# Layer 1's attention bias: from a 33-row matmul inside the output product to an addition on VectorE

## The chip, the cores and the metric

The kernel runs on one core of one Trainium2 chip. The metric is the device time of one execution in microseconds (us). The core has five engines that run their own instruction streams in order: TensorE (PE, with its weight loads listed apart as PEld), VectorE (DVE), ScalarE (ACT), GpSimd (POOL) and SyncE (SP), which here issues most of the DMAs.[...]

## The reference, cut to what matters

Two transformer-like layers are computed on 4096 tokens of width 256. Layer 0 is a linear attention plus a mixture of 32 experts; layer 1 is a softmax attention of 16 heads plus a mixture of 8 experts. What matters here is where the output bias `Wo_b` of layer 1's attention enters:

```python
def _L1_attn_ref(X, Wq_w, Wq_b, Wo_w, Wo_b, rms_w):
    ...
    O = O @ Wo_w.T + Wo_b
    return pre_X + O
...
xn = _layernorm(x, axis=-1)
x = x + _L1_attn_ref(xn, ...) + _L1_ffn_ref(xn, ...)
```

So the last line adds, for every token, `x + xn + (O @ Wo_w.T) + Wo_b + experts`. The bias is one row of 256 numbers, the same for all tokens, and it can be added at any place of that sum.

## The kernel before, in words

The 4096 tokens are cut into eight groups of 512 (`NG = 8`), each held as a tile of 128 partitions by four rows of 256 (`[P, TT, D]`). The program is a set of Python generators, one for each piece of work of each group. A generator yields `step(engine, cost, ...)` in front of the instructions that it issues. The class `Weave` simulates the engines with these costs, in us, and always takes the step that can begin first; that fixes the order of the instructions on each engine once and for all. A cost in a `step` is therefore no time of the chip, but it moves the order. `need` names events that must have happened, `get` and `put` take and give back buffers, `lat` is a delay until the result is there, `aside` lets the generator's next step begin without waiting for this one.

The pieces that the change and the prediction touch:

- `loads` at the start of layer 1's weights (L1659 to L1669) brings `wq`, `gate1`, `wo`, `bq`, `rms_w`, `gate_b` on SP's queue. `bq`, a row like the bias, is spread over all 128 partitions by its DMA.
- `biased` (L979 to L990) prepares the bias for TensorE: a tile of 33 rows, zero but for row 0 and row 32, holds the bias rounded to the fast matmul type in row 0 and what the rounding left in row 32. A second tile, `ones_r`, holds ones. A matmul of the two, contracted over 33 rows, adds the bias to every token.
- `combine(g)` (L1019 to L1055) closes layer 0 for a group and opens layer 1. It loads the sum so far (`xt`, L1024), adds the four gathered expert rows `yk` (L1027, gathered by POOL at L1012), takes the layer norm, stores the normed rows and their transpose (L1031, L1042), adds the normed rows to `xt` (L1044), computes the router's logits on PE, copies them (L1053) and stores `xt` as the residual of layer 1 (L1055). The router (`route1`), the scatter of the tokens to the experts (`spread`, L566) and the experts of layer 1 (L1158 on) come from there.
- `attended(g)` (L1489 to L1498) is the output product of layer 1's attention. It runs in two passes over the same four blocks of 128 tokens, one for each half of the contraction. In pass `i = 0` each block has the product's two matmul instructions and then the bias matmul; pass `i = 1` has the product alone. Both go through `into` (L865), so their instructions stand at L871.
- `closed1(g)` (L1556) loads the residual back, adds the finished PSUM banks to it by `onto` (L943), and stores it; `finish(g)` and `added` (L1539 to L1574) add the experts' rows `y1k` at the end and write the output.

The experts of layer 1 run as 39 tiles between the attention of groups 3 to 6; the attention of group 7 and all of `finish` come last.

Of the kernel before, what the change touches and what calls it, by code (L numbers as in the profile page):

```python
# [7 lines left out]
F32 = mybir.dt.float32  # L8
I32 = mybir.dt.int32
BF16 = mybir.dt.bfloat16  # L10
F32R = mybir.dt.float32r
U32 = mybir.dt.uint32
AF = mybir.ActivationFunctionType
ALU = mybir.AluOpType
# [3 lines left out]
P = 128  # L18
D = 256
# [4 lines left out]
NG = T // GT  # L24
TT = GT // P
# [25 lines left out]
C_ID, C_TRI, C_ONE, C_MASK = 0, 128, 256, 384  # L51
# [155 lines left out]
def step(eng, cost, **o):  # L207
    return eng, cost, o
# [3 lines left out]
def two_layers(  # L212
# [6 lines left out]
    nc = tc.nc  # L219
# [4 lines left out]
    def kc_rows(ap):  # L224
        return ap.rearrange("(k p) n -> p k n", p=P)

    const = ctx.enter_context(tc.tile_pool(name="const", bufs=1))
# [7 lines left out]
    w = Weave(  # L235
        dict(
            big=BIG, mid=MID, s=BANKS, o0=2, o1=1, up=1, pT=2, aT0=1, aT1=1,
            unit=2, xr=3, w=3, mt=2, wc=4, rt=1, pp=2, rt1=1, chunk=4, mix1=2,
            at0=1, at1=1, xr1=3, w1r=3, w1b=3,
        )  # L240
    )

    def big(shape, name, dtype=F32):
        return work.tile(shape, dtype, tag="big", name=name, bufs=BIG)
# [6 lines left out]
    def bank(shape, i=0):  # L251

        n = shape[1] if len(shape) == 2 else shape[1] * shape[2]
        ap = banks[w.ids["s"][i]][: shape[0], :n]
        return ap if len(shape) == 2 else ap.rearrange("p (a b) -> p a b", a=shape[1])
# [5 lines left out]
    cst = const.tile([P, C_END], F32, name="cst")  # L261
# [12 lines left out]
    g1_t = const.tile([P, KC, E1], F32, name="g1")  # L274
    wo_t = const.tile([P, KC, D], F32, name="wo")
    bq_t = const.tile([P, D], F32, name="bq")

    BR = 33
    bo_t = const.tile([BR, D], F32, name="bo")
    bo_r = const.tile([BR, D], F32R, name="bo_r")  # L280
    ones_r = const.tile([BR, P], F32R, name="ones_r")
    rw_t = const.tile([P, KC], F32, name="rw")
    gb_t = const.tile([P, E1], F32, name="gb")

# [55 lines left out]
    def load(name, lat, dst, src, eng=None):  # L340
        return name, lat, dst, src, eng
# [25 lines left out]
    def norms(xt, key, need=lambda t: []):  # L367

        st = few([P, TT, 6], "st")
        mv = few([P, TT, 2], "mv")  # L370
        for t in range(TT):
            yield step("DVE", 0.6, need=need(t))
            nc.vector.bn_stats(st[:, t, :], xt[:, t, :])
            nc.vector.bn_aggr(mv[:, t, :], st[:, t, :])
        yield step("DVE", 0.16)
        var = few([P, TT], "var")
        nc.vector.tensor_scalar(var, mv[:, :, 1], LN_EPS, None, ALU.add)
        yield step("POOL", 1.05, rush=RUSH)
        rstd = few([P, TT], "rstd")
        nc.gpsimd.tensor_tensor(rstd, var, nhalf.to_broadcast([P, TT]), ALU.pow)  # L380
        yield step("DVE", 0.16)
        off = few([P, TT], "nmr")
        nc.vector.scalar_tensor_tensor(off, mv[:, :, 0], -1.0, rstd, ALU.mult, ALU.mult)
        for t in range(TT):
            yield step("ACT", 0.6, get=["big"] if t == 0 else [])
            if t == 0:
                xn = xns[key] = big([P, TT, D], "xn")
            nc.scalar.activation(
                xn[:, t, :], xt[:, t, :], AF.Identity, bias=off[:, t : t + 1],
                scale=rstd[:, t : t + 1],  # L390
            )
        yield step("DVE", 0.5)

        ms = few([P, TT], "ms")
        nc.vector.tensor_tensor(ms, rstd, rstd, ALU.mult)
        nc.vector.tensor_tensor(ms, ms, mv[:, :, 1], ALU.mult)
        nc.vector.tensor_scalar(ms, ms, RMS_EPS, None, ALU.add)
        yield step("POOL", 1.05, aside=True, rush=RUSH, gives=[("rs", key)])
        rss[key] = few([P, TT], "rs", bufs=NG)
        nc.gpsimd.tensor_tensor(rss[key], ms, nhalf.to_broadcast([P, TT]), ALU.pow)  # L400
# [464 lines left out]
    def into(o, n, pairs):  # L865

        done = n_down.get(o, 0)
        n_down[o] = done + 1
        for t in range(2 * len(oTs[o])):
            for i, (lhs, rhs) in enumerate(pairs):  # L870
                nc.tensor.matmul(  # L871
                    oTs[o][t // 2][:, t % 2, :],
                    lhsT=lhs[:, t * P : (t + 1) * P] if lhs.shape[1] > P else lhs,
                    rhs=rhs,
                    start=(done == 0 and t % 2 == 0 and i == 0),
                    stop=(done == n - 1 and t % 2 == 1 and i == len(pairs) - 1),
                )
# [85 lines left out]
    halves, logits, aTs, aPs, ys = {}, {}, {}, {}, {}  # L963
# [12 lines left out]
                wq_t[:, k, :], wq_t[:, k, :], rw_t[:, k : k + 1], None, ALU.mult  # L976
            )

    def biased():  # L979
        yield step("DVE", 0.2)  # L980
        nc.vector.memset(bo_t, 0.0)
        yield step("SP", 0.3, lat=45.0)
        nc.sync.dma_start(bo_t[:1, :], bo)
        nc.sync.dma_start(bo_t[BR - 1 :, :], bo)
        yield step("ACT", 0.4, need=["cst"])
        nc.scalar.copy(bo_r, bo_t)
        nc.scalar.copy(ones_r, cst[:BR, C_ONE : C_ONE + P])
        yield step("DVE", 0.4, gives=["bo_r"])
        last = slice(BR - 1, BR)
        nc.vector.tensor_tensor(bo_r[last, :], bo_t[last, :], bo_r[last, :].bitcast(F32), ALU.subtract)  # L990

    def heads():
        for i in range(2):
            yield step("POOL", 2.0)
            nc.gpsimd.memset(vones[i][:, :, :, DK:], 1.0)
            yield step("POOL", 2.5)
            nc.gpsimd.memset(turned[i], 0.0)
            yield step("POOL", 0.2, gives=["heads"] if i else [])
            nc.gpsimd.memset(turned[i][:, :, :, 0:1], -1.0)
# [19 lines left out]
    def combine(g):  # L1019

        need = [("x1", g, b) for b in range(GT // S)] + ["tiles0"]
        yield step("SP", 0.4, get=["big", "mix1"], need=need, lat=2.5, gives=[("mix1", g)])
        xt = big([P, TT, D], "xt")
        nc.sync.dma_start(xt, midg[g])  # L1024
        for k in range(TOPK0):
            yield step("DVE", 1.22, need=[("y", g, k)], put=["big"])
            nc.vector.tensor_tensor(xt, xt, ys.pop((g, k)), ALU.add)  # L1027
        yield from norms(xt, NG + g)
        xn = xns[NG + g]
        yield step("SP", 0.4, aside=True, lat=2.5, gives=[("rows1", g)])  # L1030
        nc.sync.dma_start(rd1g[g], xn)  # L1031
        for k in range(KC):
            yield step("PE", 0.6, get=["s"] + (["big"] if k == 0 else []))
            if k == 0:
                xnT = big([P, KC, GT], "xnT1")
            tp = bank([P, TT, P])
            for t in range(TT):
                nc.tensor.transpose(tp[:, t, :], xn[:, t, k * P : (k + 1) * P], ident)
            yield step("ACT", 0.6, put=["s"])
            nc.scalar.copy(xnT[:, k, :], tp.rearrange("p t n -> p (t n)"))  # L1040
        yield step("SP", 0.4, aside=True, lat=2.5, gives=[("xnT1", g)])
        nc.sync.dma_start(xnT_d[g], xnT.rearrange("p k n -> p (k n)"))  # L1042
        yield step("DVE", 1.22, aside=True)
        nc.vector.tensor_tensor(xt, xt, xn, ALU.add)  # L1044
        yield step("PE", 2.0, get=["s"], need=["gate1"])
        lg = bank([P, TT, E1])
        for t in range(TT):
            matmul_k(
                lg[:, t, :], lambda k: xnT[:, k, t * P : (t + 1) * P], lambda k: g1_t[:, k, :]
            )  # L1050
        yield step("DVE", 0.2, put=["s", "big", "big"], gives=[("lg", g)])
        logits[g] = few([P, TT, E1], "lgs", bufs=NG)
        nc.vector.tensor_copy(logits[g], lg)  # L1053
        yield step("SP", 0.4, lat=2.5, put=["big", "mix1"], gives=[("res1", g)])
        nc.sync.dma_start(res1g[g], xt)  # L1055
# [430 lines left out]
    WO = KC  # L1486
    NC1 = 2

    def attended(g):  # L1489

        for i in range(WO):
            yield step(
                "PE", 1.75 if i else 2.2,
                need=[("o", NG + g), ("aT", g, 0), ("aT", g, 1), "wo", "bo_r"],
                put=["big"] if i == WO - 1 else [], gives=[("dn1", g, NC1 + i)],
            )
            bias = [] if i else [(ones_r, bo_r)]
            into(NG + g, NC1 + WO, [(aPs[g][:, i, :], wo_t[:, i, :])] + bias)  # L1498

    def chunk(g, c):  # L1500

# [155 lines left out]
    for j in range(4):  # L1657
# [5 lines left out]
            load("gate1", 45.0, g1_t, kc_rows(gate1)),  # L1663
            load("wo", 45.0, wo_t, kc_rows(wo)),
            load("bq", 45.0, bq_t, bq.partition_broadcast(P)),
            load("rms_w", 45.0, rw_t, rms_w),
            load("gate_b", 45.0, gb_t, gate_b.partition_broadcast(P)),
        ]), 50,
    )  # L1669
    w.add(scaled(), 52)  # L1670
    w.add(biased(), 53)
    w.add(heads(), 54)
    w.add(late_ring(), DENSE[-1] + 9)
    for g in range(NG):
# [97 lines left out]
```

## Time and profile before

| | us |
|---|---|
| Time, median of 3 runs (lowest to highest) | 1543.43 (1538.72 to 1546.51) |
| The profiled execution, its own time | 1544.06 |
| Its span, first to last instruction | 1542.3 |
| Granted TensorE clock over the span | 0.971 of full |
| L1044, the addition of the normed rows: 8 instructions | 1.217 each |
| L871, bias matmul with weight load: 32 of each | 0.381 and 0.183 each (medians) |
| L986, L987 on ACT and L981, L990 on DVE (`biased`) | 0.391, 0.296, 0.272, 0.449 |

The eight bias passes of `attended` stand at 906, 1047, 1106, 1185, 1274, 1366, 1460 and 1519 us of the span. The eight L1044 additions stand at 725, 752, 779, 847, 906, 987, 1032 and 1092 us.

How to read such a page: its first part gives each engine's busy time, its second the same over 40 slices of the span. A group's row ends in the idle time of the engine before these instructions and in what ended it. In a timeline each row is the start, the duration, the engine, the line, the operation, what it writes and reads, and the shapes; a bracket at the end is idle time before it with its releaser. Matmuls overlap one another, so the time that a matmul takes from its engine is read from start to start and not from its duration.

### The profile page before, as it was taken

How to read it: one execution, taken by the hardware profiler on the slowest of the kernel's cores; microseconds unless marked ns; L12 is line 12 of the kernel's file. 1: busy time of each engine (PE TensorE's matmuls, PEld its weight loads, DVE VectorE, ACT ScalarE, POOL GpSimd, SP SyncE). 2: the span in 40 equal slices, each digit the busy share in tenths (PEclk: the TensorE clock that was granted, in tenths of full speed). 3: DMA queues.
4: the chain of work that ended last, by engine and by line, in shares of the span. 5: the costliest groups of instructions: out<-in, count | busy, mean ns of one | idle time of the engine just before them, and what ended most of it. 6: DMA issues, size and time to landing. Idle time of an engine off the chain costs nothing.

```text
span 1542.3 us, 27989 instructions
## 1 busy us (share of the span) xinstructions
PE 1421.5 (92%) x9702; PEld 1115.6 (72%) x9702; DVE 907.4 (59%) x2421; ACT 726.1 (47%) x1585; POOL 786.7 (51%) x1062
## 2 busy tenths in 40 slices
PE   5999999999999998799889999999889999999965
PEld 3777787577788876688658888876568887777733
DVE  5987767683322233225776645577757676656662
ACT  4333222435554555433343423354566877867521
POOL 4477677545555555437667444336054655645100
PEclk9999999999999999999879999999999999999977
DMA  9211110138777788964486251325355444544393
GB/s 338 96 56 42 42 29 15 28 113 240 211 241 224 232 232 201 177 169 130 135 120 117 76 157 26 113 92 124 121 126 161 137 145 141 152 146 132 99 304 117
DMA packets 160483, 214.23 MB, mean 139 GB/s; under 512 B 29843, under 2 KB 123797, under 8 KB 160085
## 3 DMA queue, kind: packets, MB, share of 16 engines
q1 hardware_dynamic: 131140, 148.92, 31.7%
q0 software_dynamic: 29200, 63.51, 17.3%
q8 instruction: 77, 1.26, 0.3%
q14 instruction: 66, 0.53, 0.1%
HBM read 137.65 MB, written 70.19 MB: 135 GB/s over the span
## 4 chain that ended last, share of the span: by engine, by line
PE 51%; DMA 15%; DVE 4%; issue 3%; POOL 3%; ACT 2%; SPq 2%; DVEq 0%; POOLq 0%; ACTq 0%
PE bank L894 8%; PE bank L871 8%; DMA xr_ring<-rows_d,who 7%; PE bank L350 6%; PE bank L1184 4%; PE bank L1350 3%; PE bank L1361 3%; PE bank L749 3%; PE bank L1407 3%; PE bank L1426 3%; PE bank L1211 2%; PE bank L731 2%; PE bank L1511 1%; POOL xr_ring L715 1%; DMA y1k<-y 1%
## 5 line engine op out<-in xcount | busy, mean ns | idle before, releaser
L715 POOL DMA_INDIRECT xr_ring<-rows_d,who x190 | 181.2, 954 | 163.7 <-PE bank L731 123.1
L566 POOL DMA_INDIRECT perm<-pairs,at_u x192 | 194.3, 1012 | 98.5 <-issue 33.0
L894 PE MATMUL bank<-yT,wsw 128*128 128x256 f32 x1024 | 238.9, 381 | 0.0
L894 PEld LDWEIGHTS bank<-yT,wsw 128*128 128x128 f32 x1024 | 193.2, 191 | 29.2 <-issue 4.0
L736 DVE COPY xTr<-bank 128x512 f32<-128x512 f32 x95 | 65.1, 687 | 175.6 <-PE bank L731 161.0
L1012 POOL DMA_INDIRECT yk<-y,slots x128 | 133.4, 1042 | 61.2 <-issue 34.3
L1372 DVE TENSOR_REDUCE tops<-bank 128x3 f32<-128x384 f32 x256 | 131.4, 548 | 50.4 <-PE bank L1350 50.2
L1419 ACT ACTIVATE pT<-bank 128x384 f32<-128x384 f32 x256 | 111.7, 495 | 93.4 <-PE bank L1350 89.9
L1232 POOL DMA_INDIRECT y<-ry,to x78 | 79.3, 1017 | 109.1 <-ACT ry L1221 78.3
L871 PE MATMUL bank<-wdn,sg 128*128 128x256 f32 x512 | 125.5, 391 | 5.8 <-DVE sg L920 5.8
L871 PEld LDWEIGHTS bank<-wdn,sg 128*128 128x128 f32 x512 | 98.7, 197 | 24.0 <-DVE sg L920 6.1
L759 ACT ACTIVATE ry<-bank,share 128x256 f32<-128x256 f32 x190 | 79.5, 470 | 69.5 <-PE bank L749 67.9
L350 PE MATMUL bank<-xTr,w_ring 128*128 128x256 f32 x380 | 99.3, 386 | 3.3 <-DMA w_ring<-in_wud 2.1
L749 PE MATMUL bank<-w_ring,ra 128*128 128x256 f32 x380 | 98.2, 382 | 0.0
L916 ACT ACTIVATE sg<-bank 128x512 f32<-128x512 f32 x64 | 38.2, 596 | 127.4 <-PE bank L894 127.3
L1140 POOL DMA_INDIRECT xr<-rows_d,who x78 | 81.3, 1043 | 25.4 <-issue 16.8
L350 PE MATMUL bank<-wqkvsu,xnT 128*128 128x512 f32 (+1 forms) x256 | 91.6, 492 | 0.0
L1361 PE MATMUL bank<-kT,qT 32*128 32x128 f32 (+1 forms) x1024 | 77.3, 368 | 11.3 <-DVE at L534 4.0
L1407 PE MATMUL bank<-qT,kT 32*128 32x256 f32 (+1 forms) x1024 | 70.0, 359 | 15.4 <-DVE tops L1372 12.7
L731 PE MATMUL bank<-cst,xr_ring 128*128 128x128 f32 x380 | 62.8, 280 | 22.8 <-DMA xr_ring<-rows_d,who 20.5
L1184 PE MATMUL bank<-xhi,w_ring 128*88 128x256 f32 x312 | 80.5, 292 | 1.2 <-ACT ry L1221 0.7
L743 ACT ACTIVATE ra<-bank 128x256 f32<-128x256 f32 x95 | 36.4, 383 | 95.3 <-PE bank L350 90.0
(257 smaller groups left out, 3128.0 us busy)
## 6 DMA issues: line engine op xcount, KB each, us to landing
w_ring<-in_wud SPq DMA_DIRECT2D x95, 256.0 KB
y<-ry SPq DMA_DIRECT2D x95, 256.0 KB
w_b<-in_we SPq DMA_DIRECT2D x39, 304.0 KB
rows_d<-xn SPq DMA_DIRECT2D x16, 512.0 KB
xnT<-xnT_d SPq DMA_DIRECT2D x16, 512.0 KB
y1k<-y SPq DMA_DIRECT2D x16, 512.0 KB
x<-in_x SPq DMA_DIRECT2D x8, 512.0 KB
res_d<-x SPq DMA_DIRECT2D x8, 512.0 KB
```

The costliest lines, as they stand in the source:

```text
L350: nc.tensor.matmul(ps_ap, lhsT=lhs(k), rhs=rhs(k), start=(k == 0), stop=(k == KC - 1))
L566: ins = nc.gpsimd.indirect_dma_start(out=la.perm, out_offset=bass.IndirectOffsetOnAxis(ap=la.at_u[:, c : c + 1], axis=0), in_=la.pairs[:, ...
L715: nc.gpsimd.indirect_dma_start(out=xr_ring[:, m % 3, i * D : (i + 1) * D], out_offset=None, in_=rows_d, in_offset=bass.IndirectOffsetOnAxi ...
L749: nc.tensor.matmul(o[:, i, :], lhsT=a[:, i * P : (i + 1) * P], rhs=wt[:, 2 * I0 :], start=True, stop=True,)
L871: nc.tensor.matmul(oTs[o][t // 2][:, t % 2, :], lhsT=lhs[:, t * P : (t + 1) * P] if lhs.shape[1] > P else lhs, rhs=rhs, start=(done == 0 a ...
L894: nc.tensor.matmul(ap[:, i, :], lhsT=w_of[0](i, k), rhs=rhs[:, k, :], start=(i == 0 and k == 0), stop=(i == 1 and k == KC - 1),)
L1012: nc.gpsimd.indirect_dma_start(out=ys[g, k][:, t, :], out_offset=None, in_=y0, in_offset=bass.IndirectOffsetOnAxis(ap=L0.slots[:, c : c + ...
L1184: nc.tensor.matmul(h[:, c, :], lhsT=w_c(i // 2), rhs=(hi, lo)[i % 2][:, i // 2, :], start=(i == 0), stop=(i == n - 1),)
L1361: nc.tensor.matmul(four[r][:, i * P : i * P + n], lhsT=qT[rows_of(r), c, i * P : (i + 1) * P], rhs=kT[rows_of(r), c, :n], start=(i == 0), ...
L1372: nc.vector.tensor_reduce(tops[b][:, c * 4 + r, :], four[r].rearrange("p (i n) -> p i n", n=P), AX.X, ALU.max,)
L1407: nc.tensor.matmul(four[r][:, q : q + n], lhsT=kT[rows_of(r), c, i * P : (i + 1) * P], rhs=mT[rows_of(r), c, i * P :], start=(i == 0), sto ...
L1419: nc.scalar.activation(pT[:, :, r, :], four[r].rearrange("p (b n) -> p b n", n=P), AF.Exp)
```

## The change

The bias is no longer part of the output product. It is loaded like `bq`, spread over 128 partitions; in `combine(g)`, right behind the addition of the normed rows, a second addition of the same shape on VectorE adds it to the residual, before that is stored. `biased`, its 33-row tiles, its two small DMAs and the 32 bias matmuls go, with the event `bo_r`; the planned cost of pass `i = 0` becomes that of pass `i = 1`.

```diff
-
-    BR = 33
-    bo_t = const.tile([BR, D], F32, name="bo")
-    bo_r = const.tile([BR, D], F32R, name="bo_r")
-    ones_r = const.tile([BR, P], F32R, name="ones_r")
+    bo_t = const.tile([P, D], F32, name="bo")
...
-    def biased():
-        yield step("DVE", 0.2)
-        nc.vector.memset(bo_t, 0.0)
-        yield step("SP", 0.3, lat=45.0)
-        nc.sync.dma_start(bo_t[:1, :], bo)
-        nc.sync.dma_start(bo_t[BR - 1 :, :], bo)
-        yield step("ACT", 0.4, need=["cst"])
-        nc.scalar.copy(bo_r, bo_t)
-        nc.scalar.copy(ones_r, cst[:BR, C_ONE : C_ONE + P])
-        yield step("DVE", 0.4, gives=["bo_r"])
-        last = slice(BR - 1, BR)
-        nc.vector.tensor_tensor(bo_r[last, :], bo_t[last, :], bo_r[last, :].bitcast(F32), ALU.subtract)
-
...
         yield step("DVE", 1.22, aside=True)
         nc.vector.tensor_tensor(xt, xt, xn, ALU.add)
+
+        yield step("DVE", 1.22, aside=True, need=["bo"])
+        nc.vector.tensor_tensor(xt, xt, bo_t.unsqueeze(1).to_broadcast([P, TT, D]), ALU.add)
         yield step("PE", 2.0, get=["s"], need=["gate1"])
...
             yield step(
-                "PE", 1.75 if i else 2.2,
-                need=[("o", NG + g), ("aT", g, 0), ("aT", g, 1), "wo", "bo_r"],
+                "PE", 1.75,
+                need=[("o", NG + g), ("aT", g, 0), ("aT", g, 1), "wo"],
                 put=["big"] if i == WO - 1 else [], gives=[("dn1", g, NC1 + i)],
             )
-            bias = [] if i else [(ones_r, bo_r)]
-            into(NG + g, NC1 + WO, [(aPs[g][:, i, :], wo_t[:, i, :])] + bias)
+            into(NG + g, NC1 + WO, [(aPs[g][:, i, :], wo_t[:, i, :])])
...
             load("bq", 45.0, bq_t, bq.partition_broadcast(P)),
+            load("bo", 45.0, bo_t, bo.partition_broadcast(P)),
...
-    w.add(biased(), 53)
...
-        "bo": a["L1_attn_Wo_b"].reshape(1, D),
+        "bo": a["L1_attn_Wo_b"],
```

## The prediction

> **What bounds the kernel now.** I read the busy shares first, then the busy time by stretches, because both halves of the change sit late in the span.
>
> ```profile
> PE 1421.5 (92%) x9702; PEld 1115.6 (72%) x9702; DVE 907.4 (59%) x2421; ACT 726.1 (47%) x1585; POOL 786.7 (51%) x1062
> ```
>
> TensorE is busy 92% of the span, but an average hides the stages. The windows (length, then busy time of PE, PEld, DVE, ACT, POOL, the clock and the DMA) separate them:
>
> ```profile
> 725.00:900.00 175.00, 159.24 (x1111) 125.08 (x1110) 118.94 (x389) 69.39 (x133) 111.31 (x137) 0.91 0.54 117
> ...
> 814.00:1020.00 206.00, 204.96 (x1422) 167.38 (x1425) 120.96 (x354) 76.33 (x149) 87.44 (x111) 1.00 0.38 97
> 1020.00:1150.00 130.00, 116.40 (x1212) 79.41 (x1212) 90.67 (x286) 71.67 (x147) 57.38 (x79) 0.97 0.45 121
> 1150.00:1462.00 312.00, 305.53 (x2997) 247.14 (x2998) 208.95 (x392) 221.11 (x430) 162.68 (x234) 1.00 0.44 136
> 1462.00:1543.00 81.00, 48.05 (x347) 29.27 (x346) 34.21 (x49) 16.86 (x38) 0.15 (x1) 0.75 0.67 214
> ```
>
> From 814 to 1020 TensorE idles 1 us in 206, from 1150 to 1462 it idles 6.5 in 312: whatever it is spared there moves everything behind it forward. From 1020 to 1150 it idles 13.6 of 130. The last 81 us are a tail of waits. Ahead of 814 lies a stretch where VectorE and the gathers set the pace: the waits of TensorE list 4.0 us for L534 at 756 and 4.6 us for the maxima (L1372) at 795, both held up on VectorE behind an L1027 addition that waits for a DMA.
>
> **What is removed from TensorE.** The timeline of one bias pass and of the pass without a bias, group 5:
>
> ```profile
> 1365.63 0.60 PE L871 MATMUL bank<-wo,aP 128*128 128x256 f32 x2
> 1366.16 0.38 PE L871 MATMUL bank<-bo_r,ones_r 33*128 33x256 f32 x1
> 1366.47 0.70 PE L871 MATMUL bank<-wo,aP 128*128 128x256 f32 x2
> 1367.10 0.38 PE L871 MATMUL bank<-bo_r,ones_r 33*128 33x256 f32 x1
> ...
> 1369.29 0.66 PE L1162 MATMUL bank<-cst,xr 128*128 128x128 f32 x4
> ...
> 1369.79 1.89 PE L871 MATMUL bank<-wo,aP 128*128 128x256 f32 x8
> ...
> 1371.52 1.03 PE L350 MATMUL bank<-wq,xnT 128*128 128x256 f32 x4
> ```
>
> The bias pass holds the engine from 1365.63 to 1369.29, 3.66 us; the other pass from 1369.79 to 1371.52, 1.73 us. The difference, 1.93 us, is four bias matmuls, 0.48 us each, several times the 0.12 us that the 88-row matmuls of L1211 at 1364.73 to 1365.08 take from start to start. The weight-load rows say why:
>
> ```profile
> 1366.16 0.18 PEld L871 LDWEIGHTS bank<-bo_r,ones_r 33*128 33x128 f32 x1 [0.33 <-issue]
> ```
>
> The bias weights are not loaded during the matmul ahead; the loader idles 0.33 us, and in the whole trace 11.2 us before these 32 loads. **A rule to weigh here:** the Trainium skill, "TensorE: Matmul & The Clock Gate", section Back-to-back issue gap, gives a matmul of 256 columns 262 cycles at 2.4 GHz, 0.109 us. By it 32 bias matmuls are an estimated 3.5 us, and the change would buy nothing after its additions. "TensorEngine Tiling", section Key Properties, says that changing the tiling mode drains the engine; 33 rows among 128-row matmuls would be such a change. The start-to-start row decides: 0.48.
>
> By group:
> - Groups 0 and 3 to 6 (906, 1185, 1274, 1366, 1460) lie where TensorE has no gaps: 5 x 1.93 = 9.65 us, all counted.
> - Groups 1 and 2 (1047, 1106) lie in the stretch with 13.6 us of idle time, where the way to the first expert tile (route, eight scatters by POOL, gather) is a chain of latencies: between 0 and 3.86 us. I take half, 1.93, as the stretch is 90% busy but ends in a wait for a gather.
> - Group 7: the first two bias matmuls stand at 1519.35 and 1520.30 ahead of a 10.18 us wait for `aP` (L1480), so they are hidden and worth nothing. The last two, at 1532.01 and 1533.67, are on the final chain. The clock is half there: a block starts every 1.66 us with a bias and every 0.85 us without, so 2 x 0.81 = 1.62 us.
>
> Sum: 9.65 + 1.93 + 1.62 = **13.2 us gained**, between 11.3 and 15.1.
>
> **What is added to VectorE.** Eight additions like L1044, both inputs in SBUF:
>
> ```profile
> L1044 DVE TENSOR_TENSOR xt<-xt,xn 128x1024 f32<-128x1024 f32 x8 | 9.7, 1216 | 0.0
> ```
>
> L1044 starts at 725.39 and the next VectorE instruction at 726.52, so one costs its queue 1.13 us; 8 x 1.13 = 9.0 us if nothing covers it. Queued behind each on VectorE are the logits' copy (L1053), with the router behind it, and pieces of the attention that TensorE waits for; on SP the residual's store (L1055) waits, and whatever SP has queued behind that. In the 12 us behind the eight places VectorE is busy 8.2, 7.4, 10.2, 8.2, 5.9, 8.1, 9.4 and 11.2 us.
> - Groups 3 to 6 have 2.6 to 6.1 us of slack there, and TensorE runs on: 0 (each 1.13 if the cover fails).
> - Group 7 at 1092 has 0.8 us of slack in 12, with TensorE already waiting for `sh` and `hlo`: 1.13.
> - Group 2 at 779: VectorE is nearly full, and SP issues the load of the next `xt` (780.39) just behind the residual's store (779.94); VectorE later idles 4.76 us for that load. Late by one or the other: 1.13.
> - Groups 0 and 1 at 726 and 752: VectorE then idles 2.05 and 3.40 us for gathered rows, so its queue absorbs 1.13. **Here a rule speaks against the change:** the skill's "SBUF — State Buffer", section Who interferes with whom, says that a VectorE instruction with two SBUF inputs contends with a GpSimd instruction that reads SBUF. The trace agrees:
>
> ```profile
> 733.99 0.95 POOL L1012 DMA_INDIRECT yk<-y,slots  x1 [0.30 <-issue]
> 735.25 1.87 POOL L1012 DMA_INDIRECT yk<-y,slots  x1 [0.30 <-issue]
> ...
> 735.07 1.23 DVE L1027 TENSOR_TENSOR xt<-xt,yk 128x1024 f32<-128x1024 f32 x1 [2.05 <-DMA yk<-y,slots]
> ```
>
> A gather beside such an addition takes 1.87 instead of 0.95 us. Without this, groups 0 and 1 cost 0; with it 0.92 each, since the chain of waits runs through exactly these gathers (727 to 759). I take 1.84.
>
> Sum: 1.13 + 1.13 + 1.84 = **4.1 us lost**, between 0 and 9.0 + 1.84 = 10.8.
>
> **The rest.** At the start go 0.27 and 0.45 us of VectorE, 0.69 us of ACT and two DMA issues (0.31 and 0.23 us on SP); one issue like `bq`'s (0.71 us) comes. These lie beside a TensorE that is 92% busy over the first 300 us: 0, between 1.4 us gained and 0.2 lost. The event `bo` comes some 45 planned us after the start, `combine` begins at 680: its wait costs nothing. Every order is re-planned: the planner takes 0.45 off TensorE and adds 1.22 to VectorE in each group, and the logits' step can be taken only after the new one. No row shows what a new order costs. The nearest bound is the idle time of TensorE behind 725 (15.8, 6.6, 13.5 and 33 us in the windows up to 900, 1100, 1460 and the end), which an order can shrink or stretch. I take 0, with 8 us to either side for the range.
>
> **Sum:** 13.2 - 4.1 = 9.1 us. The profiled execution had a span of 1542.3 and a time of 1544.06, so 1535.0 for it; it lies 0.6 us above the median, which gives **1534.4**.
>
> **The rivals.**
> - *More of it* (chance 0.15): groups 1 and 2 count in full and VectorE's slack hides all additions: 1543.4 - 15.1 = 1528.3. For it: the DVE shares above. Against it: the gathers.
> - *No gain* (0.15): expert tiles and attention are paced by something that hides behind a seemingly full TensorE, such as the weights' way (w_b, then the cast L1127) or the gathers; only group 7's 1.62 us remains, less part of the additions: 1543. For it: ACT is busy 221 of 312 us there and the chain of waits visits L1127. Against it: every wait of TensorE there is below 1.8 us.
> - *Slower* (0.20): the new order puts more of the closing transfers ahead of group 7's own on SP's queue. In the tail TensorE waits 10.2, 7.7 and 4.1 us for what comes through that queue; a 512 KB transfer there takes 1.72 us at the slice's 304 GB/s. Six more of them ahead of group 7's sums and shares undo the gain, and from eleven the kernel is slower beyond doubt: 1534.4 + 11 x 1.72 = 1553. For it: 28 such transfers are due in the tail, in an order that only the planner's costs set. Against it: the change moves the planner little there.
>
> **How the numbers follow.** The forecast case has 0.50 (its own range 1527 to 1541). A measurement tells about 0.5%, 7.7 us, from no change, so the line is at 1535.7; the forecast is close to it, and about 0.35 of its 0.50 lies below. Faster: 0.35 + 0.15 = 0.50. Same: 0.15 + 0.15 = 0.30. Slower: 0.20. The range runs from below the first rival with a lucky order, 1522, to the middle of the slower rival, 1551.
>
> **What would show it.** No `bo_r` rows at L871; both passes of `attended` at 1.73 us; about 13 us less between the first bias pass and the end of TensorE's full stretch; 16 instead of 8 additions at L1044 and the new line, 1.13 us apart; gathers of 1.87 us beside the new ones. The forecast is wrong if the first 800 us grow by more than 3 us, if the first expert tile doesn't start earlier, or if the tail behind the last expert tile is longer than 81 us.

## The result, and the profile after

| | us |
|---|---|
| Time before, median of 15 runs (lowest to highest) | 1540.37 (1532.31 to 1547.58) |
| Time after, median of 15 runs | 1534.53 (1528.12 to 1537.97) |
| Ratio, with its 95% interval | 0.9954 (0.9935 to 0.9972) |
| The profiled execution of after, its own time, span, clock | 1533.85, 1532.0, 0.971 |

The change gains about 7.1 us: 0.46% of 1540.37, with 4.3 to 10.0 as the interval; the medians alone lie 5.8 us apart. The forecast was a gain of 9.1 us and a time of 1534.4.

The busy shares of after, from its page:

```profile
PE 1412.7 (92%) x9670; PEld 1115.0 (73%) x9670; DVE 913.0 (60%) x2427; ACT 725.4 (47%) x1583; POOL 783.0 (51%) x1062
```

TensorE has 32 instructions fewer (9702 before) and is busy 8.8 us less; VectorE has eight additions more, less the two preparing instructions, and is busy 5.6 us more.

Because the order of all work is new, windows at fixed times would compare different work. I therefore cut both executions at the same three events: layer 0's last matmul with `wdn` and `hs`, layer 1's first expert matmul (L1184 before), its last expert matmul (L1211 before). The columns are the window, its length, then busy time of PE, PEld, DVE, ACT and POOL, the granted clock, the DMA share and GB/s. First before, then after:

```profile
0.00:1019.10 1019.10, 950.63 (x5143) 759.11 (x5144) 572.91 (x1695) 416.44 (x971) 565.60 (x749) 0.98 0.50 136
1019.10:1150.60 131.50, 117.61 (x1222) 80.38 (x1220) 91.85 (x288) 71.92 (x147) 58.84 (x80) 0.97 0.45 121
1150.60:1442.40 291.80, 286.45 (x2838) 233.47 (x2836) 196.69 (x369) 210.25 (x407) 159.90 (x229) 1.00 0.45 138
1442.40:1542.30 99.90, 66.82 (x507) 42.63 (x505) 45.95 (x72) 27.53 (x60) 2.34 (x5) 0.80 0.62 194
```

```profile
0.00:1016.20 1016.20, 947.69 (x5118) 755.42 (x5119) 576.81 (x1694) 415.03 (x965) 563.25 (x747) 0.98 0.48 137
1016.20:1151.30 135.10, 123.83 (x1266) 85.23 (x1265) 95.04 (x295) 74.69 (x156) 57.92 (x82) 0.96 0.45 118
1151.30:1437.20 285.90, 278.17 (x2772) 231.32 (x2771) 194.01 (x362) 208.20 (x403) 159.48 (x229) 0.99 0.45 141
1437.20:1532.00 94.80, 62.99 (x519) 42.98 (x518) 47.18 (x78) 27.52 (x60) 2.35 (x5) 0.84 0.65 204
```

By stage after is 2.9 us shorter, 3.6 longer, 5.9 shorter and 5.1 shorter. The second stage gives back more than the first one has won, so the first expert matmul starts at 1151.3 instead of 1150.6. And the instruction counts of a stage differ (1266 against 1222 matmuls in the second): work has moved across the events. It has: even the longest common sequence, with instructions told apart by line, operation, names and shapes, leaves only 7965 of TensorE's 9670 instructions and 1999 of VectorE's 2427 in the same succession as before. Two things were changed at once, work and order; the experiments part them.

The additions themselves, in VectorE's timeline of after, and their groups (count, then busy time and mean ns):

```profile
724.47 1.22 DVE L1027 TENSOR_TENSOR xt<-xt,xn 128x1024 f32<-128x1024 f32 x1
725.60 1.22 DVE L1010 TENSOR_TENSOR xt<-xt,yk 128x1024 f32<-128x1024 f32 x1
726.74 1.22 DVE L1030 TENSOR_TENSOR xt<-xt,bo 128x1024 f32<-128x1024 f32 x1
```

```profile
L1030 DVE TENSOR_TENSOR xt<-xt,bo 128x1024 f32<-128x1024 f32 x8 | 9.8, 1220 | 0.1
L1027 DVE TENSOR_TENSOR xt<-xt,xn 128x1024 f32<-128x1024 f32 x8 | 9.7, 1216 | 0.0
```

L1027 is the old L1044, and L1010 the old L1027; L1030 is new. In group 0 the two additions are not neighbours: the planner has set another group's addition between them, and each takes its queue 1.13 to 1.14 us from start to start, as estimated. Where they are neighbours, in groups 2, 3 and 7, the second works on what the first has just written, and the first then holds the queue 1.25 us.

### The profile page after: what moved, and what is told of

It reads as the page before. It is cut to its first block, busy times and chain, and to the rows that moved or that the text cites. A ratio compares the mean times of both kernels' runs of the same rounds, so it can differ in the third digit from the quotient of the medians.

```text
span 1532.0 us, 27865 instructions
## 1 busy us (share of the span) xinstructions
PE 1412.7 (92%) x9670; PEld 1115.0 (73%) x9670; DVE 913.0 (60%) x2427; ACT 725.4 (47%) x1583; POOL 783.0 (51%) x1062
## 3 DMA queue, kind: packets, MB, share of 16 engines
q8 instruction: 76, 1.25, 0.3%
## 4 chain that ended last, share of the span: by engine, by line
PE 62%; DMA 13%; DVE 10%; POOL 4%; issue 4%; SPq 3%; ACT 3%; DVEq 0%; ACTq 0%; POOLq 0%
PE bank L890 14%; PE bank L867 11%; PE bank L346 9%; DMA xr_ring<-rows_d,who 6%; PE bank L1170 4%; PE bank L745 3%; PE bank L1347 3%; PE bank L1336 3%; PE bank L828 2%; PE bank L1393 2%; PE bank L1197 2%; PE bank L727 2%; PE bank L1412 2%; DMA yk<-y,slots 2%; POOL xr_ring L711 1%
## 5 line engine op out<-in xcount | busy, mean ns | idle before, releaser
L562 POOL DMA_INDIRECT perm<-pairs,at_u x192 | 191.1, 995 | 79.6 <-issue 32.3
L995 POOL DMA_INDIRECT yk<-y,slots x128 | 131.8, 1029 | 59.7 <-issue 33.0
L1126 POOL DMA_INDIRECT xr<-rows_d,who x78 | 80.5, 1032 | 28.2 <-issue 18.8
L1347 PE MATMUL bank<-kT,qT 32*128 32x128 f32 (+1 forms) x1024 | 82.9, 380 | 12.7 <-DVE r L939 7.6
L346 PEld LDWEIGHTS bank<-xTr,w_ring 128*128 128x128 f32 x380 | 68.2, 190 | 18.9 <-issue 6.6
```

Source lines behind the costliest of these rows:

```text
L346: nc.tensor.matmul(ps_ap, lhsT=lhs(k), rhs=rhs(k), start=(k == 0), stop=(k == KC - 1))
L562: ins = nc.gpsimd.indirect_dma_start(out=la.perm, out_offset=bass.IndirectOffsetOnAxis(ap=la.at_u[:, c : c + 1], axis=0), in_=la.pairs[:, ...
L995: nc.gpsimd.indirect_dma_start(out=ys[g, k][:, t, :], out_offset=None, in_=y0, in_offset=bass.IndirectOffsetOnAxis(ap=L0.slots[:, c : c + ...
L1347: nc.tensor.matmul(four[r][:, i * P : i * P + n], lhsT=qT[rows_of(r), c, i * P : (i + 1) * P], rhs=kT[rows_of(r), c, :n], start=(i == 0), ...
```

## The experiments

All ratios are to the kernel before on the same chip, in five rounds, with 95% intervals. The runs fell on three chips. On two of them the kernel before takes 1776.0 us (e1 to e4) and 1759.3 us (e9 to e12), on the third 1545.5 us (e5 to e8). Only ratios are compared across chips; what the profile shows of the difference is told at the end.

### The removal alone, the addition alone, both in the old order, and a bias of 128 rows

e1 takes only the bias matmuls out of `attended`; everything else, the order too, is that of before. The bias is missing from its result.

```diff
-            bias = [] if i else [(ones_r, bo_r)]
+            bias = []
```

> The kernel before with its order of instructions unchanged; only the 32 bias matmuls are left out, so the output lacks layer 1's output bias. This is the gain of the removal alone. Theory of the prediction: 13.2 us faster than before (11.3 to 15.1), most of it between the first bias pass and the end of TensorE's full stretch. Rival 'no gain' (experts and attention are paced by something other than TensorE): 1 to 2 us faster. Rival by the 262-cycle rule: 3.5 us faster.

Measured: 1763.58 us, ratio 0.9929 (0.9899 to 0.9959): 12.6 us gained (7.3 to 17.9).

e2 leaves the matmuls in and adds a second addition in the step of L1044. Its row is `bq`'s, which is already there, so its result carries that row too.

```diff
         nc.vector.tensor_tensor(xt, xt, xn, ALU.add)
+        nc.vector.tensor_tensor(xt, xt, bq_t.unsqueeze(1).to_broadcast([P, TT, D]), ALU.add)
```

> The kernel before with its order unchanged and its bias matmuls kept; behind each of the eight L1044 additions stands a second one of the same shape, which adds the query bias row (so the output has a row too many). This is the cost of the additions alone. Theory of the prediction: 4.1 us slower than before, of it 3.0 in the stretch from 725 to 800. If VectorE's slack hides all: 0. If nothing hides them: 9.0 to 10.8 slower.

Measured: 1775.36 us, ratio 1.0008 (0.9984 to 1.0032): 1.4 us lost (2.8 gained to 5.7 lost). The median is even a little below before's 1776.03; neither is clear of zero.

e3 makes the whole change, but keeps every `step` with its cost and so the order of before: the addition stands in the step of L1044, the load in that of the two small DMAs.

```diff
+    bo_t = const.tile([P, D], F32, name="bo")
...
-        nc.sync.dma_start(bo_t[:1, :], bo)
-        nc.sync.dma_start(bo_t[BR - 1 :, :], bo)
+        nc.sync.dma_start(bo_t, bo.partition_broadcast(P))
...
         nc.vector.tensor_tensor(xt, xt, xn, ALU.add)
+        nc.vector.tensor_tensor(xt, xt, bo_t.unsqueeze(1).to_broadcast([P, TT, D]), ALU.add)
         yield step("PE", 2.0, get=["s"], need=["gate1"])
...
                 "PE", 1.75 if i else 2.2,
...
+            bias = []
```

> The whole change, but with the order of the kernel before: the addition stands in the same planned step as L1044, and no planned cost is changed. Theory: the sum of the two parts, 9.1 us faster than before, and so some 2 us faster than the re-planned kernel after if the new order costs anything. If it is as fast as the kernel after within 2 us, the new order is worth nothing either way.

Measured: 1763.51 us, ratio 0.9933 (0.9909 to 0.9957). Between e1 and e3 lie 0.04%, 0.7 us of 1776: the addition in the old order costs nothing that these runs can tell, though the two intervals together leave some 7 us to either side.

e4 asks why a bias matmul is dear. It keeps the bias on TensorE in the same places and with the same type, and only fills the 33 rows up to 128 with zeros.

```diff
-    BR = 33
+    BR = 128
...
-        nc.sync.dma_start(bo_t[BR - 1 :, :], bo)
+        nc.sync.dma_start(bo_t[32:33, :], bo)
...
-        last = slice(BR - 1, BR)
+        last = slice(32, 33)
```

> The kernel before with its order unchanged, but the bias tile and the tile of ones have 128 rows instead of 33 (rows of zeros added, the second part of the bias in row 32). If the 0.48 us of a bias matmul is the price of switching between 33 and 128 rows, it falls to about 0.12 us, the start-to-start time of the 88-row matmuls of the same type, and the kernel is 4 x 8 x 0.36 = 11.5 us less on TensorE, so some 9 us faster than before without any addition on VectorE. If it is the price of the change of number type from f32 to f32r and back, the pass stays at 3.66 us and the time stays the same.

Measured: 1767.99 us, ratio 0.9957 (0.9938 to 0.9977): 7.6 us gained (4.1 to 11.0) by matmuls that multiply more zeros. The change of number type is still there, so it was not that. TensorE's timeline of e4, one bias pass, the rows between the second and the last block left out:

```profile
1586.81 0.60 PE L871 MATMUL bank<-wo,aP 128*128 128x256 f32 x2
1587.05 0.47 PE L871 MATMUL bank<-bo_r,ones_r 128*128 128x256 f32 x1
1587.36 0.59 PE L871 MATMUL bank<-wo,aP 128*128 128x256 f32 x2
...
1589.01 0.60 PE L1162 MATMUL bank<-cst,xr 128*128 128x128 f32 x4
```

The pass runs from 1586.81 to 1589.01, 2.20 us, where it was 3.66. Above the 1.73 us of a pass without a bias that leaves 0.117 us for a bias matmul instead of 0.48. Both figures are differences of passes and not rows: from a bias matmul to the next one it is 0.31 us here and in before (1366.16 to 1366.47). The time is lost ahead of it, 0.53 to 0.63 us from a block's first product matmul to its bias matmul in before, 0.24 in e4. The loader shows the same, in the group of the bias weights; the last column is the loader's idle time before them. Before and e4:

```profile
L871 PEld LDWEIGHTS bank<-bo_r,ones_r 33*128 33x128 f32 x32 | 6.1, 189 | 11.2 <-issue 11.2
```

```profile
L871 PEld LDWEIGHTS bank<-bo_r,ones_r 128*128 128x128 f32 x32 | 7.1, 222 | 1.6 <-issue 0.3
```

The idle time falls from 11.2 to 1.6 us, though each load has become slightly longer. (On e4's own chip, e2 shows 11.3 for the 33-row loads.) What is dear is the change between 33 and 128 rows, not the matmul. It is not any change of the row count: the expert matmuls of before go from 128 to 88 rows and back at 0.11 to 0.12 us from start to start.

```profile
1435.97 0.28 PE L1184 MATMUL bank<-xlo,w_ring 128*88 128x256 f32 x1
1436.09 0.28 PE L1211 MATMUL bank<-w_ring,thi 88*128 88x256 f32 x1
...
1436.92 0.28 PE L1211 MATMUL bank<-w_ring,tlo 88*128 88x256 f32 x1
1437.03 0.28 PE L1184 MATMUL bank<-xhi,w_ring 128*88 128x256 f32 x1
```

### The order

Four kernels ran together on the fast chip: the changed kernel (e6), the same work in the old order (e7, which is e3 again), and two with a single planned cost altered. e5 is the kernel before with

```diff
-                "PE", 1.75 if i else 2.2,
+                "PE", 1.75,
```

so that not one instruction is other than before, only their order. e8 is the changed kernel with this line put back.

> The kernel after, as it is, beside e7 on the same chip. Theory: its parts are worth what they were in the old order (removal about 0.7% of the time, additions about 0.1% at most), so it is 0.5 to 0.7% faster than before, and any shortfall against e7 is the price of the new order. If the new order costs nothing, it equals e7 within 0.2%.

> The whole change in the old order, a second time, as the partner of e6 on the same chip. Theory: 0.6 to 0.7% faster than before, as in e3. If e3 was a lucky reading, it comes out near the 0.46% of the kernel after.

> The kernel before with all its work, the bias matmuls too; only the planned cost of the first pass of the output product is 1.75 instead of 2.2, so the order of all engines is planned anew. Nothing is computed differently. If orders are worth nothing, the time is that of before within 0.2%. If a new order by itself moves the time by several us, as the slower rival of the prediction needs, it shows here: 0.3% or more either way.

> The kernel after with one planned cost put back (2.2 for the first pass, though the bias matmul is gone): the same work as the kernel after in one more order. Theory that orders matter by some us at random: it differs from the kernel after by up to 0.4%, in either direction. Theory that they don't: within 0.2% of it.

| | work | planned cost of the first pass | median us | ratio to before | us at clock 0.966 |
|---|---|---|---|---|---|
| before | old | 2.2 | 1545.54 | 1 | 1545.1 |
| e5 | old | 1.75 | 1552.07 | 1.0040 (1.0021 to 1.0059) | 1550.3 |
| e6 = after | new | 1.75 | 1537.61 | 0.9949 (0.9932 to 0.9966) | 1538.9 |
| e8 | new | 2.2 | 1529.90 | 0.9910 (0.9884 to 0.9936) | 1530.9 |
| e7 | new, every step of before | 2.2 | 1531.57 | 0.9907 (0.9877 to 0.9938) | 1532.3 |

The last column takes the clock out. Within a kernel, a run with a mean clock 0.01 higher is 9.1 us shorter (a line through all 113 runs of the five kernels on this chip, each about its own mean; that the clock is the cause is not shown). With each kernel's mean brought to one clock along this line, the distances remain: e5 loses 5.2 us to before, and e6 loses 8.0 us to e8. On this chip the number 1.75 in place of 2.2 thus costs 5 to 8 us whichever work is planned. With 2.2 the new step and the new load cost nothing: e8 and e7 are alike.

Where does the order lose it? The windows of e7 and e5, cut at the same events as above:

```profile
0.00:1014.50 1014.50, 948.12 (x5139) 756.81 (x5140) 579.48 (x1699) 415.98 (x969) 565.87 (x749) 0.98 0.50 137
1014.50:1145.90 131.40, 119.71 (x1214) 83.42 (x1212) 93.90 (x289) 71.93 (x147) 58.77 (x80) 0.93 0.45 121
1145.90:1432.00 286.10, 281.30 (x2825) 233.48 (x2824) 196.89 (x369) 210.55 (x407) 160.31 (x230) 0.99 0.46 141
1432.00:1529.00 97.00, 61.44 (x499) 40.70 (x497) 45.74 (x72) 27.59 (x60) 2.35 (x5) 0.78 0.63 200
```

```profile
0.00:1019.80 1019.80, 952.31 (x5143) 758.81 (x5144) 572.44 (x1695) 416.17 (x971) 564.99 (x749) 0.98 0.50 136
1019.80:1159.90 140.10, 125.77 (x1250) 84.70 (x1248) 92.29 (x287) 73.23 (x151) 58.01 (x80) 0.90 0.43 114
1159.90:1455.20 295.30, 288.03 (x2793) 235.03 (x2792) 196.62 (x369) 208.85 (x402) 157.19 (x229) 0.98 0.44 137
1455.20:1555.90 100.70, 69.95 (x523) 44.01 (x521) 46.15 (x72) 27.79 (x61) 2.34 (x5) 0.79 0.62 192
```

The second stage looks like the place: 131.5 us before, 140.1 in e5, 135.1 in after, 131.4 in e7. But read the clock with it. In e5 it is 0.90 there, before it was 0.97: 140.1 x 0.90 is 126.1 us at full clock, 131.5 x 0.97 is 127.6 (an estimate, as if all of the stage went with the clock). In this one execution the clock would be enough to explain the whole stage; e8, the fastest, has 142.2 us at 0.90 there and makes it good with 80.5 us behind the last expert matmul. That the order costs 5 to 8 us is measured; **at which instruction it does so stays open.** One profile for each kernel, with a clock that drops in different stretches, doesn't tell.

What the old order with the new work shows stage by stage is cleaner, as the counts agree. Before to e7: 4.6 us, 0.1, 5.7 and 2.9 shorter. The third stage holds the bias passes of groups 3, 4 and 5, expected at 3 x 1.93 = 5.8. It is one execution of each kernel, though, and those of before alone spread over 15 us, so the agreement to 0.1 us is partly luck.

### Other planned costs

If 2.2 is better than 1.75, is more better still? e9 and e10 plan the first pass of the changed kernel at 2.0 and 2.4; e11 is the kernel before, planned with 3.66, what its pass really takes.

```diff
-                "PE", 1.75,
+                "PE", 1.75 if i else 2.0,
```

> The kernel after with 2.0 instead of 1.75 as the planned cost of the first pass; the same work in one more order. If the 0.4 to 0.5% between e6 (1.75) and e8 (2.2) comes from a value that is too small, 2.0 lies between them: 0.6 to 0.8% faster than before. If it is chance of the order, 2.0 may land anywhere from 0.2 to 1.1% faster.

> The same with 2.4. If a larger planned cost is better in itself, it is at least as fast as e8: 0.9% faster than before or more. If it is chance, anywhere from 0.2 to 1.1%.

> The kernel before, bias matmuls included, with the planned cost of the first pass set to what the trace shows, 3.66 instead of 2.2. If an order planned with a truer cost is better, it is 0.3% or more faster than before. If order is chance, it is anywhere within 0.5% of before on either side.

Measured: e9 0.9995 (0.9963 to 1.0027), e10 0.9969 (0.9936 to 1.0001), e11 0.9959 (0.9929 to 0.9990). The true cost helps the kernel before by 0.4% with no work changed; yet in the changed kernel the nearly true cost of 1.75 loses to 2.2. There is no direction in it. e9 missed both of its expectations, 0.6 to 0.8% and 0.2 to 1.1% faster; e10 falls short of e8's 0.9%; e11 fits both of its theories and so decides nothing. The size of a move of this number, about 0.4%, is what repeats (e5, e6 against e8, e11). As e8 didn't run on this chip, e9 and e10 don't say that 2.2 is the best value.

### How much VectorE can take

e12 is e3 with two more additions of the `bq` row behind each bias addition: sixteen more, and its result carries that row twice.

```diff
         nc.vector.tensor_tensor(xt, xt, bo_t.unsqueeze(1).to_broadcast([P, TT, D]), ALU.add)
+        nc.vector.tensor_tensor(xt, xt, bq_t.unsqueeze(1).to_broadcast([P, TT, D]), ALU.add)
+        nc.vector.tensor_tensor(xt, xt, bq_t.unsqueeze(1).to_broadcast([P, TT, D]), ALU.add)
```

> The whole change in the old order (e3 and e7, 0.67 and 0.93% faster than before), but each bias addition is followed by two more additions of a row, of the query bias, so the output has two rows too many; 16 more instructions of 1.13 us, 18 us of VectorE. If VectorE's slack hides the additions, most of these are hidden too: no more than 5 us slower than e3 and e7, so still 0.4 to 0.7% faster than before. By the prediction's count (groups 0 to 2 and 7 pay, the slack of groups 3 to 6 is used up at the third) they cost 8 to 12 us: about as fast as before. If none is hidden, 18 us: 0.3 to 0.5% slower than before.

Measured: 1768.50 us, ratio 1.0046 (1.0018 to 1.0074), against 0.9933 for e3 on another chip: the sixteen cost about 1.13%, 20 us of 1759 (13 to 26 by the two intervals). VectorE's timeline of e12 shows what they take from its queue: each one that reads what the last wrote starts 1.26 us behind it, so 16 x 1.26 = 20 us, not 18.

```profile
782.37 1.22 DVE L1036 TENSOR_TENSOR xt<-xt,xn 128x1024 f32<-128x1024 f32 x1
783.61 1.22 DVE L1037 TENSOR_TENSOR xt<-xt,bo 128x1024 f32<-128x1024 f32 x1
784.87 1.23 DVE L1038 TENSOR_TENSOR xt<-xt,bq 128x1024 f32<-128x1024 f32 x1
786.13 1.23 DVE L1039 TENSOR_TENSOR xt<-xt,bq 128x1024 f32<-128x1024 f32 x1
787.27 1.28 DVE L1019 TENSOR_TENSOR xt<-xt,yk 128x1024 f32<-128x1024 f32 x1
```

The first addition of a group is free within what e2 and e3 can tell, the second and third are paid about in full. Some of the slack can be seen in the group of the additions of gathered rows, e3 and then e12; the last column is VectorE's idle time before them:

```profile
L1019 DVE TENSOR_TENSOR xt<-xt,yk 128x1024 f32<-128x1024 f32 x32 | 39.1, 1223 | 7.7 <-DMA yk<-y,slots 6.3 <-DMA xt<-mid_d 1.4
```

```profile
L1019 DVE TENSOR_TENSOR xt<-xt,yk 128x1024 f32<-128x1024 f32 x32 | 39.1, 1222 | 3.0 <-DMA yk<-y,slots 2.3 <-issue 0.6
```

In e3 VectorE still waits 6.3 us for gathered rows, in e12 only 2.3. These 4 us are a small part of the 20, so what else the first addition hides in was not shown.

## Why the prediction came out as it did

The sum was 13.2 - 4.1 + 0 = 9.1 us. The cause it named, the removal from TensorE, is the one that gained. Two of its three terms were mis-sized, in opposite directions, and the total came out 2 us off: that it is so close is partly luck. The predicted time, 1534.4 against 1534.53, is luck outright: it was counted from the median of three runs, 3.1 us above the later median of fifteen, and that just made up for the smaller gain.

**The removal, 13.2 us: right.** Alone it measured 12.6 (7.3 to 17.9). The rule weighed there, the skill's "TensorE: Matmul & The Clock Gate", section Back-to-back issue gap, with 262 cycles or 0.109 us for a 256-column matmul, would have made it 3.5 us, below the interval. The difference of the passes, 0.48 us, decided, and e4 shows the cause: with 128 rows the same bias matmul costs 0.117 us, close to that rule. The rule does not fit every matmul here: the product's own, of the other number type, take 0.216 us each in pass `i = 1` (eight in 1.73). The 0.36 us on top of the 0.117 come with 33 rows among 128. That fits the Trainium skill's "TensorEngine Tiling", section Key Properties, which says that a change of tiling mode drains TensorE; that such a drain is what takes them, no run here shows. Group by group, in the old order and in one execution each: groups 3 to 5 gave 5.7 of the 5.8 predicted. The last stage, groups 6 and 7, gave 2.9 of 1.93 + 1.62 = 3.55. The stage that holds groups 1 and 2, for which I took 1.93, shows 0.1, at a clock of 0.93 against 0.97, so this guess stays untested. The first stage, with group 0's pass and six of the additions, gave 4.6, more than the 1.93 of that pass; where the rest comes from is not shown.

**The additions, 4.1 us lost: mis-sized.** Measured 1.4 us (2.8 gained to 5.7 lost) by e2, 0.7 by e3 less e1. VectorE's queue gives up more than was counted, 1.26 us for each addition in the old order, since it stands right behind L1044 (1.25 and 1.14 instead of 1.13). The measured intervals include 4.1; that the true cost is near zero rests on both estimates and on three readings of the rows:

- *Group 2, 1.13 us for a load behind the residual's store.* In e7 the load of the next `xt` was issued at 780.83 us instead of 780.39 (behind L1044 it is 1.26 us later, as foreseen), and the wait of 4.76 us for it, which I let the addition lengthen, is gone. Its landing was not set by when the addition ended. Before and e7, the first instruction that uses this load:

```profile
797.93 1.23 DVE L1027 TENSOR_TENSOR xt<-xt,yk 128x1024 f32<-128x1024 f32 x1 [4.76 <-DMA xt<-mid_d]
```

```profile
793.97 1.23 DVE L1019 TENSOR_TENSOR xt<-xt,yk 128x1024 f32<-128x1024 f32 x1
```

- *Groups 0 and 1, 0.92 us each for a gather beside the addition.* Long gathers are there; after has one of 1.94 us beside additions at 754.67 (an old one, of gathered rows) and 755.80 (a new one):

```profile
753.49 0.95 POOL L995 DMA_INDIRECT yk<-y,slots  x1 [0.30 <-issue]
754.75 1.94 POOL L995 DMA_INDIRECT yk<-y,slots  x1 [0.31 <-issue]
```

  But a gather is held up by whichever such addition it meets, and it meets some anyway. All 128 took 133.4 us before, 131.8 after and 132.6 in e7, with the old order; with 16 additions more than e3's, in e12, they took 129.0, where e3 has 128.9. Gathers of over 1.3 us number 10 before, 9 after and 11 in e7. Before, after and e7:

```profile
L1012 POOL DMA_INDIRECT yk<-y,slots x128 | 133.4, 1042 | 61.2 <-issue 34.3 <-DMA y<-ry 20.7 <-DVE at L534 3.5
```

```profile
L995 POOL DMA_INDIRECT yk<-y,slots x128 | 131.8, 1029 | 59.7 <-issue 33.0 <-DMA y<-ry 22.4 <-ACT pT L1405 0.6
```

```profile
L1004 POOL DMA_INDIRECT yk<-y,slots x128 | 132.6, 1036 | 58.8 <-issue 34.5 <-DMA y<-ry 21.1 <-DMA yk<-y,slots 0.9
```

  So the rule that spoke against the change, the skill's "SBUF — State Buffer", section Who interferes with whom, is borne out in the single gather and absent from the sum. The error was to count each new meeting as an added one.
- *Group 7, 1.13 us.* The logits are copied 1.26 us later behind L1044 in e7, yet the first expert matmul follows L1044 by 58.0 us, against 58.3 before: the copy does not end that stretch.

The step that costs groups 3 to 6 at nothing fits all this; e12 gives the price if the cover goes, about 1.2 us for each addition (0.8 to 1.6), where 1.13 was named.

**The rest, the new order taken at 0 with 8 us to either side: mis-sized.** This is the step that was furthest off. The order costs 5 to 8 us, inside the bound but near its end. I wrote that the planner takes 0.45 off TensorE in each group and passed on; that number, and not the added step, is what moved the kernel. The place I named for a loss, the closing transfers on SP's queue in the tail (the slower rival), was not it: the stage behind the last expert matmul got shorter, 94.8 us against 99.9.

**The signs named in advance.** No `bo_r` rows: so. Of the three signs against the forecast one occurred: the first expert tile didn't start earlier. It was a poor sign: in e8, the fastest kernel on its chip, the first expert matmul starts later still, at 1156.5. The first 800 us show no growth: group 3's old L1044 stands at 840.9 against 847, though group 2's went from 779 to 803. And from group 6's output product to the end it is 78.3 us, against 83.4.

**A better version.** On one chip e7 (0.9907) and e8 (0.9910) stand ahead of after (0.9949). Both are the change itself; e8 is after with one number put back, and gains 13.9 us by its ratio (9.9 to 17.9) where after gains 7.9. The intervals of e8 and after just touch (0.9936 and 0.9932).

## What to carry to other kernels

Price a matmul of 33 rows among 128-row ones by the pass with it less the pass without it, not by its size and not by its own row. Filled up with zeros it can be cheaper. An addition on an engine with slack gained a little more here, 0.67% (e3) against 0.43% (e4), but the intervals overlap, and it was free only once per group. In a kernel whose order comes from planned costs, a change of work and a change of such a number are two changes: measure them apart, and try the work with the old numbers first, since a number alone was worth as much here as half the edit.

## What the runs showed of the hardware

Two of the three chips run the kernel before in 1776 and 1759 us where the third takes 1545. The instructions compared last as long as before (L1044 1.216 us in before and in e1); the mean clock in the profiles is 0.92 instead of 0.97, and ACT and VectorE sit idle in pieces of 10 to 20 us that the profile ascribes to "remote", to no semaphore of this core. From the timeline of e3:

```profile
222.91 0.60 ACT L928 ACTIVATE hs<-bank 128x512 f32<-128x512 f32 x1 [16.91 <-remote]
...
1002.75 0.59 ACT L1515 ACTIVATE sh<-bank 88x512 f32<-88x512 f32 x1 [20.10 <-remote]
```

In e1 to e4 they come to 171 to 192 us on ACT and 95 to 99 us on VectorE; the profiles of before, of after and of e5 to e8 have none. What stops the engines there is not shown.
